# A cross-attention kernel whose first loads are dealt out anew over two DMA queues

## The chip, the core and the metric

One Trainium2 chip, one NeuronCore. The time is device microseconds for one launch of the whole kernel, inputs and output in the chip's memory. All arithmetic is in 32-bit floating point.

## What is computed

Two batches of 2048 tokens with 640 channels attend, with 20 heads of 32 channels, to 154 context rows of 1024 channels. The first 77 rows are text, the last 77 are image prompts with weights of their own; the two softmaxes are separate and their results are added. Then comes the output projection with its bias, and the input is added back.

```
text, ip = ctx[:, :77], ctx[:, 77:]
q    = heads(x @ Wq.T)
k, v = heads(text @ Wk.T), heads(text @ Wv.T)
k_ip, v_ip = heads(ip @ Wk_ip.T), heads(ip @ Wv_ip.T)
out  = softmax(q k.T / sqrt(32)) v  +  softmax(q k_ip.T / sqrt(32)) v_ip
out  = out @ Wo.T + bo + x
```

## The kernel before

Everything lies transposed, channels on the 128 partitions. The 640 channels of a token are five slices of 128 channels (`NC` = 5; "slice k" below), the 1024 context channels eight. Tokens go in blocks of 512 (`TB`); four blocks (`xs[0]` to `xs[3]`) hold the first batch. The 640 query channels are made in five column blocks of Wq (four heads each).

The work on the engines stands in one order, written out by hand as a list of words (`SCHEDULE`, L592): each word emits the instructions of one step, and every engine runs its own in that order. `q.u.h` makes queries of step `u` and block `h` (TensorE, L205, five slices), `cq` scales them (ScalarE, L219), `k` and `v` project keys and values (TensorE, L143, eight slices), `R` makes scores (L241), `K` copies them out, `M`, `S`, `E`, `D`, `I`, `N`, `T` are the steps of the softmax on VectorE, GpSimd and ScalarE, `A` multiplies by the values (L340), and the later words are the output projection. The change does not touch this list. Its first words are `R0.0`, the first scores, and `q.0.1`, which needs x's second block.

Ahead of the list stands a stretch without words, in this order:

- Loads are issued by two engines, SyncE (SP) and ScalarE (ACT); each has a DMA queue of its own. `queues` is the pair `nc.sync, nc.scalar`. `load_x` (L174) takes the next 128-channel slice of x (256 KB); `load_first` (L537) takes one slice of Wq's first column blocks (64 KB a column block); `load_ctx` (L544) takes half of the context (308 KB); `load_w(n)` (L133) takes one block of 512 KB of the key and value weights, in the order Wk, Wk_ip, Wv, Wv_ip for each column block.
- Slice 0 of the first x block comes as two halves of 256 tokens (`SIDES`, L550), 128 KB each.
- TensorE runs five matmuls on zeros (L572). Then it makes the queries of the first block for the first two column blocks together: slice 0 in four matmuls of 256 tokens (L576: column block 0 and 1 on the left half, then on the right half), slices 1 to 4 with 512 tokens (L205). A 32-bit matmul shows as two instructions in the trace.
- ScalarE scales both results. TensorE then projects the first block of Wk, needing both halves of the context, and the first of Wk_ip (`project_kv(0)`, `project_kv(1)`, L143); ScalarE copies each to `kT` (L589), and `R0.0` can begin.

In the kernel before, the halves of x's slice 0 went one to SP and one to ACT, and both column blocks of Wq's slice 0 to ACT, as two transfers of 64 KB, one ahead of and one behind that half of x. Slices 1 and 3 of x went to ACT with Wq's on SP, slices 2 and 4 the other way round. The context went to SP, the first blocks of Wk and Wk_ip to ACT, and x's second block to SP right behind the context.

Of the kernel before, what the change touches and what calls it, by code (L numbers as in the profile page):

```python
# [20 lines left out]
def kernel(  # L21
# [25 lines left out]
    nc = tc.nc  # L47
    P = 128
# [28 lines left out]
    SIDES = slice(0, HT), slice(HT, TB)  # L77
# [12 lines left out]
    xs = [const.tile([P, NC, TB], F32, name=f"x_{n}") for n in range(NHB)]  # L90
# [35 lines left out]
    wlist = [(src, c) for c in range(NC) for src in (WkT, WkipT, WvT, WvipT)]  # L126
    loaded = {}

    def load_w(n, queue=nc.sync):

        src, c = wlist[n]
        w = wslots[n % len(wslots)]
        queue.dma_start(out=w, in_=src[:, ts(c, P)].rearrange("(k p) o -> p k o", p=P))  # L133
        loaded[n] = w

    def keys_in(ps):
# [33 lines left out]
    def load_x(queue=nc.sync):  # L170

        if slices:
            i, k = slices.pop(0)
            queue.dma_start(out=xs[i][:, k], in_=xT[ts(k, P), ts(i, TB)])  # L174
# [358 lines left out]
    queues = nc.sync, nc.scalar  # L533
    slices.pop(0)

    def load_first(queue, k, c, m=3):
        queue.dma_start(  # L537
            out=wq_first[:, k, c:m].rearrange("p c o -> p (c o)"), in_=WqT[ts(k, P), c * P : m * P]
        )

    half = NCC // 2

    def load_ctx(k):
        nc.sync.dma_start(  # L544
            out=wo_ct[:, ds(k * B * LT, half * B * LT)].rearrange("p (k n) -> p k n", k=half),
            in_=ctxT[ds(k * P, half * P), :].rearrange("(k p) n -> p k n", p=P),
        )

    for n, cols in enumerate(SIDES):
        queues[n].dma_start(out=xs[0][:, 0, cols], in_=xT[:P, cols])  # L550
        load_first(nc.scalar, 0, n, n + 1)
    for k in range(1, NC):
        load_x(queues[k % 2])
        load_first(queues[1 - k % 2], k, 0, 2)
    for k in (0, half):
        load_ctx(k)
        load_w(k // half, nc.scalar)
    for _ in range(NC):
        load_x()
    nc.sync.dma_start(out=wq_first[:, :, 2], in_=WqT[:, ts(2, P)].rearrange("(k p) o -> p k o", p=P))  # L560
    for _ in range(NC):
        load_x()
    load_w(2)
    load_w(3)
    for _ in range(NC):
        load_x()
# [236 lines left out]
    for c, stages in enumerate(chains_of):  # L803
        for _, text in stages:
            for _, t in terms(text):
                for h in range(NH):
                    o = int(t[0]), NH * int(t[1]) + h
# [128 lines left out]
```

## Time and profile before

| | |
|---|---|
| median of 3 runs | 501.47 us (501.07 to 502.48) |
| the profiled execution | 502.49 us, of which the span of instructions is 500.7 us |
| TensorE clock granted, mean | 0.997 |
| TensorE matmuls (PE) | 491.0 us busy, 98% of the span |
| VectorE (DVE), GpSimd (POOL), ScalarE (ACT) | 412.7, 370.4, 301.1 us busy |
| DMA | 69.38 MB, mean 139 GB/s; 2.23 MB of it issued by ACT (q10), the rest nearly all by SP (q1) |

Times in the profile are microseconds from the start of the span. PE is TensorE's matmuls, PEld its weight loads, which overlap them. ACTq and SPq are the two engines as issuers of DMAs. `L205` is a line of the kernel. `x24` counts instructions. In brackets stands the idle time ahead of a group and what ended it. In the views of DMA the last number of a row is the time from the issue to the landing. The context lies in the tile `wo_ct` and the first Wq and key weights lie in `aT`, whose room is used otherwise later; the names in the trace are those of the tiles.

### The profile page before, as it was taken

How to read it: one execution, taken by the hardware profiler on the slowest of the kernel's cores; microseconds unless marked ns; L12 is line 12 of the kernel's file. 1: busy time of each engine (PE TensorE's matmuls, PEld its weight loads, DVE VectorE, ACT ScalarE, POOL GpSimd, SP SyncE). 2: the span in 40 equal slices, each digit the busy share in tenths (PEclk: the TensorE clock that was granted, in tenths of full speed). 3: DMA queues.
4: the chain of work that ended last, by engine and by line, in shares of the span. 5: the costliest groups of instructions: out<-in, count | busy, mean ns of one | idle time of the engine just before them, and what ended most of it. 6: DMA issues, size and time to landing. Idle time of an engine off the chain costs nothing.

```text
span 500.7 us, 10393 instructions
## 1 busy us (share of the span) xinstructions
PE 491.0 (98%) x4116; PEld 289.8 (58%) x4116; DVE 412.7 (82%) x418; ACT 301.1 (60%) x929; POOL 370.4 (74%) x158
## 2 busy tenths in 40 slices
PE   7899999999999999999999999999999999999997
PEld 4556648458457557446556654755665586444443
DVE  0039998997999999979979796777899888999886
ACT  1156666987776778768899869586666963100000
POOL 0039998889988989979976697465888999249820
PEclk8999999999999999999999999999999999999999
DMA  8993322341523534497662359444551131511125
GB/s 276 313 283 106 77 61 83 93 112 55 128 64 134 155 119 146 129 329 257 195 200 78 116 133 320 151 126 136 167 173 44 43 108 43 170 42 43 43 84 209
DMA packets 67249, 69.38 MB, mean 139 GB/s; under 512 B 5504, under 2 KB 47232, under 8 KB 67200
## 3 DMA queue, kind: packets, MB, share of 16 engines
q1 hardware_dynamic: 63968, 66.49, 42.4%
q10 hardware_dynamic: 3232, 2.23, 1.5%
q8 instruction: 32, 0.52, 0.4%
q14 instruction: 17, 0.14, 0.1%
HBM read 54.94 MB, written 10.49 MB: 131 GB/s over the span
## 4 chain that ended last, share of the span: by engine, by line
PE 90%; DMA 6%; DVE 2%; issue 0%; ACTq 0%; SPq 0%; ACT 0%; DVEq 0%
PE bank L205 32%; PE bank L887 11%; PE bank L241 10%; PE bank L340 10%; PE bank L498 10%; PE bank L143 8%; PE bank L479 6%; PE bank L508 3%; DMA aT<-in_L_xattn_Wk_ip_dram 3%; DMA acc<-in_x_dram 2%; DMA x<-in_x_dram 1%; DMA aT<-in_L_xattn_Wq_dram 1%; DVE mx L289 1%; DVE mx L292 0%; DVE pb L331 0%
## 5 line engine op out<-in xcount | busy, mean ns | idle before, releaser
L324 POOL TENSOR_TENSOR pb<-pb,rden 128x1848 f32<-128x1848 f32 (+1 forms) x60 | 175.9, 2943 | 25.8 <-DVE rden L319 24.1
L303 POOL TENSOR_TENSOR pb<-pb,mx 128x1848 f32<-128x1848 f32 (+1 forms) x42 | 128.3, 3067 | 63.2 <-PE bank L205 31.5
L205 PE MATMUL bank<-x,wq 128*128 128x512 f32 x280 | 125.8, 598 | 0.1
L289 DVE TENSOR_REDUCE mx<-pb 128x24 f32<-128x1848 f32 (+1 forms) x51 | 93.8, 1849 | 35.7 <-ACT pb L253 35.4
L331 DVE STREAM_TRANSPOSE pb<-pb 128x1920 f32<-128x1920 f32 (+1 forms) x60 | 115.5, 1934 | 6.8 <-POOL pb L324 6.8
L314 DVE TENSOR_REDUCE den<-pb 128x24 f32<-128x1848 f32 (+1 forms) x49 | 91.5, 1873 | 18.5 <-ACT pb L309 15.7
L253 ACT COPY pb<-bank 128x462 f32<-128x462 f32 (+1 forms) x204 | 87.1, 538 | 32.3 <-PE bank L241 31.7
L205 PEld LDWEIGHTS bank<-x,wq 128*128 128x128 f32 x280 | 51.5, 190 | 60.3 <-issue 59.4
L309 ACT ACTIVATE pb<-pb 128x1848 f32<-128x1848 f32 (+1 forms) x42 | 69.4, 1653 | 19.6 <-POOL pb L303 19.5
L277 ACT ACTIVATE pb<-bank,mx 128x77 f32<-128x77 f32 x184 | 53.1, 382 | 11.8 <-DVE mx L292 11.8
L340 PE MATMUL bank<-pb,v 32*32 32x512 f32 x1600 | 55.2, 597 | 0.0
L205 PE MATMUL bank<-x,aT 128*128 128x512 f32 x116 | 53.4, 610 | 0.0
L241 PEld LDWEIGHTS bank<-kT,qT 32*128 32x128 f32 x1024 | 36.5, 184 | 22.6 <-issue 15.5
L277 ACT ACTIVATE pb<-pb,mx 128x77 f32<-128x77 f32 x160 | 47.3, 374 | 0.0
L143 PE MATMUL bank<-wo_ct,aT 128*128 128x154 f32 x320 | 45.7, 297 | 1.2 <-DMA aT<-in_L_xattn_Wk_ip_dram 1.2
L241 PE MATMUL bank<-kT,qT 32*128 32x154 f32 x1024 | 45.8, 307 | 1.0 <-ACT qT L219 0.7
L143 PEld LDWEIGHTS bank<-wo_ct,aT 128*128 128x128 f32 x320 | 42.8, 188 | 4.2 <-issue 2.2
L340 PEld LDWEIGHTS bank<-pb,v 32*32 32x32 f32 x1600 | 30.8, 103 | 21.5 <-issue 9.1
L277 ACT ACTIVATION_READ_ACCUMULATOR pb<-bank,mx 128x1 f32 x144 | 37.0, 260 | 0.0
L205 PEld LDWEIGHTS bank<-x,aT 128*128 128x128 f32 x116 | 22.1, 196 | 24.8 <-issue 22.7
L479 PE MATMUL bank<-aT,wo_ct 128*128 128x512 f32 x80 | 36.4, 595 | 0.0
L219 ACT ACTIVATE qT<-bank 128x512 f32<-128x512 f32 x32 | 19.5, 619 | 27.3 <-PE bank L205 27.3
(83 smaller groups left out, 511.9 us busy)
## 6 DMA issues: line engine op xcount, KB each, us to landing
x<-in_x_dram SPq DMA_DIRECT2D x20, 1280.0 KB, 7.1
out_dram<-acc SPq DMA_DIRECT2D x19, 256.0 KB, 2.7
x<-in_x_dram SPq DMA_DIRECT2D x17, 256.0 KB, 5.9
acc<-in_x_dram SPq DMA_DIRECT2D x16, 256.0 KB, 3.4
out_dram<-x SPq DMA_DIRECT2D x15, 256.0 KB, 2.0
v<-vS SPq DMA_DIRECT2D x160, 20.0 KB, 2.2
aT<-in_L_xattn_Wv_dram SPq DMA_DIRECT2D x5, 512.0 KB, 4.1
aT<-in_L_xattn_Wv_ip_dram SPq DMA_DIRECT2D x5, 512.0 KB, 4.2
```

Source lines behind the costliest of these rows:

```text
L143: nc.tensor.matmul(keys_in(out), loaded[n][:, k, :], cT[:, k, :, t, :], start=(k == 0), stop=(k == NCC - 1))
L205: nc.tensor.matmul(pq, weight_of(q)[:, k, :], xs[place_of(u, h)][:, k, :], start=(k == 0), stop=(k == NC - 1), skip_group_check=loose,)
L241: nc.tensor.matmul(ps[g][:, ts(t, 2 * L)], qTs[(u, h)][g * D : (g + 1) * D, ts(st, P)], kT[g * D : (g + 1) * D, c, b].rearrange("p t l -> ...
L253: nc.scalar.copy(keys_of(u, s)[:, :, g], ps[g][:, : n * 2 * L].rearrange("p (n l) -> p n l", n=n))
L277: nc.scalar.activation(row, row if ps is None else rows_in(ps[g], n)[:, t, x], AF.Exp, bias=maxs[(u, s)][:, *one], accum_out=None if den i ...
L289: nc.vector.tensor_reduce(mx, rows_of(u, s), AX.X, ALU.max, negate=negate)
L303: nc.gpsimd.tensor_tensor(rows_of(u, s), rows_of(u, s), maxs[(u, s)].unsqueeze(3).to_broadcast([P, n, 2, L]), ALU.subtract)
L309: nc.scalar.activation(e, e, AF.Exp)
L314: nc.vector.tensor_reduce(den_of(u, s), rows_of(u, s), AX.X, ALU.add)
L324: nc.gpsimd.tensor_tensor(rows_of(u, s), rows_of(u, s), rdens[(u, s)].unsqueeze(3).to_broadcast([P, n, 2, L]), ALU.mult)
L331: nc.vector.transpose(p, p)
L340: nc.tensor.matmul(pa[r][g * D : (g + 1) * D, :], v4s[q % 2][rows, g, k, :], zones[rows, :, g, k, :], start=(k == 0), stop=(k == NK - 1),)
```

## The change

In the first row, slice 0 of Wq is loaded for both column blocks in one transfer of 128 KB, the first on ACT; the left half of x's slice 0 stays first on SP, the right half is second on ACT. Slices 1 to 4 change sides: x's slices 1 and 3 go to SP and 2 and 4 to ACT, Wq's slices the other way round. Before slice 1 and before slice 3 each queue has the same number of bytes ahead of it: SP has 896 KB in all, ACT 1024 KB, the same totals as before. The first blocks of Wk and Wk_ip go to SP, each behind its half of the context, and so ahead of x's second block. `load_w` loses its argument for the queue. Nothing else changes: what is loaded, where to, and all that the engines compute stay as they were, in the same order.

```diff
-    def load_w(n, queue=nc.sync):
+    def load_w(n):
 
         src, c = wlist[n]
         w = wslots[n % len(wslots)]
-        queue.dma_start(out=w, in_=src[:, ts(c, P)].rearrange("(k p) o -> p k o", p=P))
+        nc.sync.dma_start(out=w, in_=src[:, ts(c, P)].rearrange("(k p) o -> p k o", p=P))
         loaded[n] = w
...
-    for n, cols in enumerate(SIDES):
-        queues[n].dma_start(out=xs[0][:, 0, cols], in_=xT[:P, cols])
-        load_first(nc.scalar, 0, n, n + 1)
+    nc.sync.dma_start(out=xs[0][:, 0, SIDES[0]], in_=xT[:P, SIDES[0]])
+    load_first(nc.scalar, 0, 0, 2)
+    nc.scalar.dma_start(out=xs[0][:, 0, SIDES[1]], in_=xT[:P, SIDES[1]])
     for k in range(1, NC):
-        load_x(queues[k % 2])
-        load_first(queues[1 - k % 2], k, 0, 2)
+        load_x(queues[1 - k % 2])
+        load_first(queues[k % 2], k, 0, 2)
     for k in (0, half):
         load_ctx(k)
-        load_w(k // half, nc.scalar)
+        load_w(k // half)
     for _ in range(NC):
         load_x()
```

The order of issue on each queue, with the size in KB:

| queue | before | after |
|---|---|---|
| SP | x0 left 128, Wq1 128, x2 256, Wq3 128, x4 256, ctx 308, ctx 308, x's second block 5 x 256, ... | x0 left 128, x1 256, Wq2 128, x3 256, Wq4 128, ctx 308, Wk 512, ctx 308, Wk_ip 512, x's second block 5 x 256, ... |
| ACT | Wq0 64, x0 right 128, Wq0 64, x1 256, Wq2 128, x3 256, Wq4 128, Wk 512, Wk_ip 512 | Wq0 128, x0 right 128, Wq1 128, x2 256, Wq3 128, x4 256 |

## The prediction

> **What bounds the kernel now.** I read the cores view first, then the chain of waits, then what TensorE itself waited for, and last the stretch up to 23 us.
>
> ```profile
> core 0: 500.7 us, clock 0.997
> ```
>
> The span is 500.7 us; the profiled execution as a whole took 502.49, so 1.79 us lie around it.
>
> ```profile
> 1.66 4.83 DMA aT<-in_L_xattn_Wq_dram
> ...
> 7.38 12.56 DMA aT<-in_L_xattn_Wk_ip_dram
> ...
> 22.67 1.07 PE bank L241 x24
> 23.73 4.50 PE bank L205 x10
> ...
> 29.98 4.49 PE bank L205 x10
> ...
> 446.63 50.66 PE bank L887 x120
> ```
>
> The chain (start, length, what) runs through two early transfers, a slice of Wq and the first block of Wk_ip. From the first scores, R0.0 at 22.67, it is almost wholly TensorE. What TensorE waited for, longest first (total, times, longest):
>
> ```profile
> PE bank L576 <- DMA aT<-in_L_xattn_Wq_dram: 1.9, 1, 1.9
> PE bank L143 <- DMA aT<-in_L_xattn_Wk_ip_dram: 1.2, 1, 1.2
> ...
> PE bank L498 <- DVE acc L529: 0.7, 1, 0.7
> PE bank L241 <- ACT qT L219: 0.7, 1, 0.7
> ```
>
> So TensorE is the bound, the two transfers are its two longest waits, and both lie ahead of 20 us. A microsecond won before 22.67 should reach the end nearly whole: VectorE, ScalarE and GpSimd take their work from R0.0 and move with it. The timeline of TensorE shows where the early time goes:
>
> ```profile
> 3.54 1.04 PE L576 MATMUL bank<-x,aT 128*128 128x256 f32 x2
> 6.53 1.84 PE L576 MATMUL bank<-x,aT 128*128 128x256 f32 x6 [1.95 <-DMA aT<-in_L_xattn_Wq_dram]
> 8.16 8.49 PE L205 MATMUL bank<-x,aT 128*128 128x512 f32 x16
> 16.49 2.27 PE L143 MATMUL bank<-wo_ct,aT 128*128 128x154 f32 x16
> 19.98 2.37 PE L143 MATMUL bank<-wo_ct,aT 128*128 128x154 f32 x16 [1.22 <-DMA aT<-in_L_xattn_Wk_ip_dram]
> ```
>
> Slice 0 (L576) starts at 3.54 with the first column block of Wq, idles 1.95 us for the second, and goes on at 6.53. Slices 1 to 4 (L205, sixteen passes) take 8.16 to 16.65 without a wait. They are slow for another reason; here are weight loads of two stretches, one per pass, and the windows (last three columns: granted clock, DMA share, GB/s):
>
> ```profile
> 9.01 0.34 PEld L205 LDWEIGHTS bank<-x,aT 128*128 128x128 f32 x1 [0.52 <-issue]
> 9.87 0.34 PEld L205 LDWEIGHTS bank<-x,aT 128*128 128x128 f32 x1 [0.52 <-issue]
> ...
> 12.20 0.19 PEld L205 LDWEIGHTS bank<-x,aT 128*128 128x128 f32 x1 [0.24 <-issue]
> 12.63 0.19 PEld L205 LDWEIGHTS bank<-x,aT 128*128 128x128 f32 x1 [0.24 <-issue]
> ```
>
> ```profile
> 7.00:8.00 1.00, 1.00 (x6) 0.88 (x5) 0.00 (x0) 0.00 (x0) 0.00 (x0) 0.84 1.06 371
> ...
> 11.00:12.00 1.00, 1.00 (x3) 0.44 (x3) 0.00 (x0) 0.00 (x0) 0.00 (x0) 0.95 1.13 310
> ```
>
> A pass takes 0.86 us near 9 and 0.43 near 12: half the clock. A window mean of 0.84 puts the fall to 0.5 at 7.68 (0.32 of the window at half), one of 0.95 puts the return at 11.1. So 3.4 us ran at half clock, a loss of 1.7 us. The fall comes 1.15 us after the idle stretch of 4.58 to 6.53; I take that idle time for its cause.
>
> **The change, part by part.** *The first row.* Every transfer needed for slice 0 to 4 keeps its bytes; they are dealt out again. The queue positions now, from the timeline of the issuing engines and from issue to landing:
>
> ```profile
> 0.73 0.41 ACTq L537 DMA_DIRECT2D aT<-in_L_xattn_Wq_dram  x1
> ...
> 1.18 0.42 SPq L537 DMA_DIRECT2D aT<-in_L_xattn_Wq_dram  x1
> ...
> 1.64 0.43 SPq L174 DMA_DIRECT2D x<-in_x_dram  x1
> ...
> 2.14 0.45 ACTq L174 DMA_DIRECT2D x<-in_x_dram  x1
> ...
> 3.52 0.34 ACTq L537 DMA_DIRECT2D aT<-in_L_xattn_Wq_dram  x1
> ...
> 4.18 0.33 ACTq L174 DMA_DIRECT2D x<-in_x_dram  x1
> ...
> 6.51 0.33 ACTq L537 DMA_DIRECT2D aT<-in_L_xattn_Wq_dram  x1
> ```
>
> ```profile
> aT<-in_L_xattn_Wq_dram ACTq DMA_DIRECT2D x1, 64.0 KB, 2.8
> ...
> aT<-in_L_xattn_Wq_dram SPq DMA_DIRECT2D x1, 128.0 KB, 2.8
> ...
> x<-in_x_dram SPq DMA_DIRECT2D x1, 256.0 KB, 4.7
> ...
> x<-in_x_dram ACTq DMA_DIRECT2D x1, 256.0 KB, 5.3
> ...
> aT<-in_L_xattn_Wq_dram ACTq DMA_DIRECT2D x1, 128.0 KB, 4.8
> ...
> x<-in_x_dram ACTq DMA_DIRECT2D x1, 256.0 KB, 6.4
> ...
> aT<-in_L_xattn_Wq_dram ACTq DMA_DIRECT2D x1, 128.0 KB, 4.7
> ```
>
> The lower fence gives the landings of the upper one, row by row. With the bytes up to and with each transfer: SP had 256 KB in at 3.98 and 512 KB at 6.34; ACT had 64 KB at 3.53, 256 KB at 6.49 (the chain's first row), 512 KB at 7.44, 640 KB at 8.32, 896 KB at 10.58 and all 1024 KB at 11.21. Now both column blocks of Wq's slice 0 are one transfer of 128 KB, first on ACT. From below it lands like the 64 KB in its place (3.53), from above like SP's second transfer of 128 KB (3.98); I take 3.6, nearer the first, since nothing is ahead of it. Its second column block then comes 2.9 us earlier than 6.49, and the 1.95 us of idling go.
>
> Slice 0 is eight passes of 256 columns: 2.1 us, between 1.72 (half of 0.43 each) and 2.45 (six took 1.84). It ends at 5.7. Slice 1 needs 384 KB of each queue. Halfway between the landings above that is 5.16 on SP and 6.97 on ACT; I take 6.1, the middle, so TensorE waits 0.4 us. Slice 2 needs 640 KB of ACT, 8.3 at the latest; TensorE is ready at 6.1 + 1.72 = 7.8 and waits 0.3 (0 to 0.5). Slice 3 needs 768 KB, between 8.32 and 10.58, say 9.45; TensorE is ready at 9.8. Slice 4 needs all 1024 KB, 11.21 at the latest, ready 11.5. With the sixteen passes at full clock, 6.88 us, the queries end at 6.1 + 6.88 + 0.3 = 13.3 (12.6 with no wait at all, 13.9 with every landing at its upper bound), against 16.65. A half-clock stretch would add up to 1.7; I take none, because the waits are now 0.4 and 0.3 us where it was 1.95. ACT's six issues cost ScalarE nothing: it has no work before the queries end. Three issues fewer, and a table load that comes earlier, lie under that same idle time.
>
> *Context, Wk and Wk_ip on SP.* They are now issued by SP, behind its 896 KB, in one row: context, Wk, context, Wk_ip, then x's second block, which ran ahead of Wk_ip on the other queue. Three windows and ACT's line of the first 10 us (packets, MB, share):
>
> ```profile
> 0.00:10.00 10.00, 7.00 (x21) 4.92 (x22) 0.17 (x1) 1.28 (x1) 0.83 (x6) 0.88 0.82 264
> 10.00:20.00 10.00, 8.78 (x32) 4.88 (x30) 0.00 (x0) 1.54 (x4) 0.00 (x0) 0.95 1.11 341
> 20.00:30.00 10.00, 9.00 (x75) 5.70 (x75) 0.00 (x0) 2.09 (x6) 0.00 (x0) 1.00 0.96 301
> ```
>
> ```profile
> q10 hardware_dynamic: 1130, 1.10, 32.0%
> ```
>
> An issue waits until the transfer eight places ahead in the order of all issues has landed: ACT's at 3.52 for the 64 KB that landed at 3.53, that at 6.51 for the block that landed at 6.49. By this count Wk's issue now waits for slice 1 of Wq (about 6.1) and Wk_ip's for slice 2 of x (8.3), while SP's queue still has its own slices to move; so its queue doesn't run dry.
>
> 2.64 MB are in by 10 us. Up to both halves of context and Wk it is 3048 KB, 3.12 MB; up to Wk_ip 3.65 MB; up to x's second block 4.96 MB. From 10 us on they move at 341 GB/s (both queues) or 301 (SP alone in the last window). A landing comes after the bytes: ACT had moved 1.10 MB by 10.0 and its 1024 KB (1.05 MB) landed at 11.21, so I add 1.5 us, an estimate from this one pair, 1.2 at least. Context and Wk land at 12.9 to 13.1, just before the queries end at 13.3; Wk_ip at 14.5 to 14.9. Wk's projection, 2.27 us, ends at 15.6, so Wk_ip is there and the wait of 1.22 us goes. From the start of Wk_ip's projection to R0.0 it is 22.67 - 19.98 = 2.69 us, unchanged. R0.0 starts at 13.3 + 2.27 + 2.69 = 18.3 instead of 22.67: 4.4 us earlier. The second block of x (4.96 MB) lands at 18.3 to 19.2; its first use was 1.06 us after R0.0, now 19.4, and its last slice is used 3.6 us later still. It is next in line to be late and has little to spare.
>
> *What follows on SP.* Its issues for x's third block, Wq's third column block, Wv and so on come in the same order. SP waited for Wk_ip before it could issue some of them; that wait falls earlier too. The third block (with Wq's columns 6.60 MB) is in at 24.7 even at 301 GB/s, and needed at 29.98 - 4.4 = 25.6.
>
> The sum: 1.95 + 1.7 + 1.22 = 4.9 removed, less 0.4 and 0.3 of new waits, gives 4.2; by the end times it is 4.4. I take 4.3, with 3.8 and 4.8 as ends: 502.49 - 4.3 = 498.2, between 497.7 and 498.7. The three runs took 502.48, 501.47 and 501.07, so the profiled execution is 1.02 us above the median. I read that as the half-clock stretch falling more or less on the path from run to run, and do not subtract it again; if it has another cause, the result is 1 us lower.
>
> **The rivals.** *Half a clock all the same.* The fall at 7.68 may come from something other than the idle stretch, or the new waits (up to 6.97 - 5.7 = 1.3 us at slice 1) may suffice for it. For it: the wait that I blame was itself only 1.95 us. Against it: TensorE would be idle 0.7 us in all. Then 1.7 us come back: 499.9 (499.4 to 500.4). The Trainium skill ("TensorE: Matmul & The Clock Gate", the table in "Why this matters for your kernels") warns only of idle gaps above about 3 us between bursts; by that rule the gap here was harmless and this rival would hold. The trace speaks against the figure, since the clock fell after a gap of 1.95 us.
>
> *The first slices come no earlier.* If 128 KB at once land as late as the second column block did, the start is paced as before and only Wk_ip's 1.22 us and a part of the first wait are won: about 501. Against it stand the 128 KB on SP that landed 2.8 us after issue.
>
> *SP alone is too slow, and x's second block is late (slower).* The place is the first use of that block, 1.06 us after R0.0. Of 4.96 MB, 2.32 are left at 10 us. The last slice is used now at 23.73 + 3.6 = 27.3; less 1.5 for landing, SP would have to need 15.8 us for them, 147 GB/s, before anything is lost against today. At 120 GB/s it would land at 30.8, and the time would be 506.0. Against it: 301 GB/s with SP alone. The Trainium skill ("DMA: Bandwidth & Descriptors", "Rules for kernel authors") holds that spreading over issuing engines brings no bandwidth, which also speaks against this rival; 301 against 341 here says a little is lost.
>
> **How the numbers follow.** About 0.3%, 1.5 us, is what a measurement of this kernel can tell from no change, so faster means below 499.97. Forecast 0.60; still better (below 497.7) 0.04; half clock 0.24, two thirds of it below 499.97 because the median may lie 1 us lower; no earlier slices 0.07; slower 0.05. Faster: 0.60 + 0.04 + 0.16 = 0.80; same: 0.08 + 0.07 = 0.15; slower 0.05. The range takes the forecast, 1 us below it for the median, and the half-clock rival: 496.8 to 500.4.
>
> **What would show it.** In the changed kernel TensorE's wait on L576 for Wq should be gone and that on L143 for Wk_ip too; L205's sixteen passes should stand 0.43 apart from the first; R0.0 should start near 18.3; the windows up to 12 us should hold a clock near 1. I am wrong if passes 0.86 apart remain (first rival), if slice 0 still starts its second half after 5 us (second), or if TensorE waits for x within L205 after 18 us (third). If R0.0 comes 4 us earlier and the end does not, a later stage had its own bound.

## The result, and the profile after

The median fell from 501.47 us to 498.26 us (497.75 to 499.36): a ratio of 0.9938, 95% interval 0.9921 to 0.9956. The forecast was 498.2 in 496.8 to 500.4. The sum behind it held less well than its total: the start won 1.1 us less than forecast, and about as much of the profiled time that the forecast started from (1.2 us) belonged to no edit.

The cores view, and what TensorE waited for in the changed kernel (the longest that are left, apart from the start):

```profile
core 0: 496.3 us, clock 1.000
```

```profile
PE bank L205 <- DMA aT<-in_L_xattn_Wq_dram: 0.7, 1, 0.7
PE bank L241 <- ACT qT L219: 0.7, 1, 0.7
PE bank L143 <- DMA aT<-in_L_xattn_Wk_ip_dram: 0.4, 1, 0.4
```

The waits of 1.9 us for Wq and 1.2 us for Wk_ip became 0.7 and 0.4. The two late waits on L498 for VectorE are not there either; that is taken up below. The timeline of TensorE and two weight loads:

```profile
3.53 2.93 PE L576 MATMUL bank<-x,aT 128*128 128x256 f32 x8
7.18 7.10 PE L205 MATMUL bank<-x,aT 128*128 128x512 f32 x16 [0.72 <-DMA aT<-in_L_xattn_Wq_dram]
14.12 2.27 PE L143 MATMUL bank<-wo_ct,aT 128*128 128x154 f32 x16
16.75 2.37 PE L143 MATMUL bank<-wo_ct,aT 128*128 128x154 f32 x16 [0.36 <-DMA aT<-in_L_xattn_Wk_ip_dram]
19.44 1.07 PE L241 MATMUL bank<-kT,qT 32*128 32x154 f32 x24 [0.31 <-ACT kT L589]
```

```profile
8.97 0.19 PEld L205 LDWEIGHTS bank<-x,aT 128*128 128x128 f32 x1 [0.24 <-issue]
9.40 0.19 PEld L205 LDWEIGHTS bank<-x,aT 128*128 128x128 f32 x1 [0.24 <-issue]
```

Slice 0 runs in one piece; the sixteen passes of slices 1 to 4 take 7.10 us instead of 8.49, 0.43 apart. R0.0 starts at 19.44 instead of 22.67: 0.98 us from the earlier start of slice 1, 1.39 from the faster passes, 0.86 from the shorter wait for Wk_ip, 3.23 in all. The chain shows what sets this stretch now:

```profile
2.14 6.20 DMA x<-in_x_dram
...
8.35 8.36 DMA aT<-in_L_xattn_Wk_ip_dram
```

It goes from x's slice 2, for whose landing the issue of Wk_ip waits, to the landing of Wk_ip at 16.71. TensorE's work does not appear in it before 16.75.

### The profile page after: what moved, and what is told of

Its sections match the earlier page's. It is cut to its first block, busy times and chain, and to the rows that moved or that the text cites. A ratio compares the mean times of both kernels' runs of the same rounds, so it can differ in the third digit from the quotient of the medians.

```text
span 496.3 us, 10391 instructions
## 1 busy us (share of the span) xinstructions
PE 489.6 (99%) x4116; PEld 289.1 (58%) x4116; DVE 412.9 (83%) x418; ACT 300.9 (61%) x929; POOL 370.4 (75%) x158
## 3 DMA queue, kind: packets, MB, share of 16 engines
q10 hardware_dynamic: 1008, 1.18, 0.7%
## 4 chain that ended last, share of the span: by engine, by line
PE 96%; DMA 3%; ACT 0%; ACTq 0%; DVE 0%; issue 0%; DVEq 0%
PE bank L205 34%; PE bank L887 11%; PE bank L340 11%; PE bank L241 11%; PE bank L498 10%; PE bank L143 9%; PE bank L479 7%; PE bank L508 3%; DMA aT<-in_L_xattn_Wk_ip_dram 2%; DMA x<-in_x_dram 1%; ACTq L537 0%; ACT qT L219 0%; ACT pb L253 0%; ACTq L551 0%; DVE acc L830 0%
## 5 line engine op out<-in xcount | busy, mean ns | idle before, releaser
L205 PE MATMUL bank<-x,aT 128*128 128x512 f32 x116 | 52.0, 597 | 0.7 <-DMA aT<-in_L_xattn_Wq_dram 0.7
L340 PEld LDWEIGHTS bank<-pb,v 32*32 32x32 f32 x1600 | 30.5, 103 | 21.8 <-issue 9.2
L205 PEld LDWEIGHTS bank<-x,aT 128*128 128x128 f32 x116 | 21.3, 189 | 24.9 <-issue 24.5
```

The source lines that it names most:

```text
L205: nc.tensor.matmul(pq, weight_of(q)[:, k, :], xs[place_of(u, h)][:, k, :], start=(k == 0), stop=(k == NC - 1), skip_group_check=loose,)
L340: nc.tensor.matmul(pa[r][g * D : (g + 1) * D, :], v4s[q % 2][rows, g, k, :], zones[rows, :, g, k, :], start=(k == 0), stop=(k == NK - 1),)
```

## The experiments

All ratios are to the kernel before, run on the same chip in turn. The place to read in each profile is the start of R0.0.

**The kernel before, again.** No edit.

> The kernel before, profiled a second time, against itself. Between the first profiles the span fell by 4.4 us, the start of R0.0 only by 3.2 (22.67 to 19.44); the other 1.2 us lie where TensorE waited for VectorE (0.7 and 0.3 us on L498). Theory: those late waits come and go from execution to execution and are no part of the change; then this profile has a span between 499.3 and 500.7 and may lack them, with R0.0 again at 22.5 to 22.8. Rival: they belong to the order of the work in the kernel before; then they stand again, 0.6 us or more together, and the change removed them by its earlier start. Both expect the half-clock stretch of 3.4 us again if the idle stretch ahead of 6.5 us causes it.

Measured: 501.57 us against 501.59, ratio 0.9996 (0.9984 to 1.0009). The second profile, cores and TensorE's timeline, and one window of a microsecond (the third number from the end is the granted clock):

```profile
core 0: 499.9 us, clock 0.999
```

```profile
7.16 2.93 PE L576 MATMUL bank<-x,aT 128*128 128x256 f32 x6 [2.57 <-DMA aT<-in_L_xattn_Wq_dram]
9.88 7.31 PE L205 MATMUL bank<-x,aT 128*128 128x512 f32 x16
...
23.06 1.07 PE L241 MATMUL bank<-kT,qT 32*128 32x154 f32 x24 [0.31 <-ACT kT L589]
```

```profile
8.00:9.00 1.00, 1.00 (x3) 0.76 (x3) 0.00 (x0) 0.38 (x1) 0.00 (x0) 1.00 1.06 393
```

R0.0 starts at 23.06, later than in the first profile (and than the 22.5 to 22.8 expected), and the span is shorter; the waits on L498 are absent. So they come and go, as the theory had it. The other part of its expectation held in another form: after an idle stretch of 2.57 us the rest of slice 0 ran at half clock (six passes of 256 columns in 2.93 us, 1.84 in the first profile), and the slow passes ended a little after 10 us. The granted clock stands at 1.00 in that window all the same: the clock changes kept with this trace begin with the rise to full clock at 10.4 us, and the column reads 1.00 ahead of the first of them. In this stretch the lengths of the passes tell the clock, not that column.

**Only the first row.** `load_w(k // half, nc.scalar)` put back; the rest as changed.

> Only the first row is dealt out anew; Wk and Wk_ip stay on the issue of ScalarE. Theory (the start of R0.0 sets the end, and it waits for the later of the queries and Wk_ip): the queries end near 14.3 us as in the changed kernel, but Wk_ip lands at 19 to 20 as before, so TensorE waits 2.5 to 3.5 us there and R0.0 starts at 22 to 22.7: the time falls by 0 to 0.7 us. Rival (the parts add up): the new row alone is worth 0.98 + 1.39 = 2.4 us, time 499.1.

Measured: 502.75 us, ratio 1.0024 (1.0010 to 1.0038). Slower, which neither expected. In TensorE's timeline:

```profile
7.26 7.11 PE L205 MATMUL bank<-x,aT 128*128 128x512 f32 x16 [0.51 <-DMA aT<-in_L_xattn_Wq_dram]
17.63 4.45 PE L143 MATMUL bank<-wo_ct,aT 128*128 128x154 f32 x32 [3.26 <-DMA aT<-in_L_xattn_Wk_dram]
```

The queries end near 14.3 us as in the changed kernel, but now Wk itself lands at 17.5 (15.3 in the first profile of before). SP had x's second block issued from 7.33 us, a microsecond earlier than before, and it shares the DMA engines with Wk on the other queue, which would explain the delay; no run takes it apart. The parts do not add up: the first row alone gains nothing. This profile is of its fastest run (501.10). Its twelve runs lie in three groups by mean granted clock: 501.1 to 501.4 us at 1.000, 502.6 to 502.8 at 0.996 to 0.997, and 503.4 to 504.3 at 0.992 to 0.993. A mean of 0.993 over 502 us is a loss of up to 3.5 us, so the slower runs are those in which the clock was down for longer; where in the span it was down, and whether the wait of 3.26 us brings it about, is not shown.

**Only the weights on SP.** In the kernel before:

```diff
-        load_w(k // half, nc.scalar)
+        load_w(k // half)
```

> Only Wk and Wk_ip go to SP ahead of x's second block; the first row stays as before. Theory: the queries end at 16.65 as before, Wk_ip is there by 17 to 18.9, so its wait of 1.22 us is gone and R0.0 starts at 21.3 to 21.8: the time falls by 0.9 to 1.3 us, to 500.2 to 500.6. The half-clock stretch stays. Rival (the parts add up): this part is worth 0.86 us, time 500.6; the two theories part on the first row alone.

Measured: 500.17 us, ratio 0.9979 (0.9963 to 0.9994): a fall of 1.4 us. The runs lie between 498.15 and 502.39. The profile is of one of the longer ones (501.57). TensorE waits there for neither Wk nor Wk_ip, but R0.0 starts at 22.94, not at the 21.3 to 21.8 expected:

```profile
7.18 2.93 PE L576 MATMUL bank<-x,aT 128*128 128x256 f32 x6 [2.62 <-DMA aT<-in_L_xattn_Wq_dram]
9.90 8.50 PE L205 MATMUL bank<-x,aT 128*128 128x512 f32 x16
18.25 4.38 PE L143 MATMUL bank<-wo_ct,aT 128*128 128x154 f32 x32
22.94 1.07 PE L241 MATMUL bank<-kT,qT 32*128 32x154 f32 x24 [0.31 <-ACT kT L589]
```

Behind an idle stretch of 2.62 us the rest of slice 0 and three to four passes of slice 1 ran at half clock. That this is what spreads the other runs is not shown.

**The same, with the idle stretch filled.**

```diff
                 pq[:, cols], wq_first[:, 0, c], xs[0][:, 0, cols], start=(n == 0), stop=False, skip_group_check=True
             )
+            if n == c == 0:
+                for _ in range(6):
+                    nc.tensor.matmul(banks[0][:, :P], warm, warm, start=True, stop=True)
```

> The same with six more matmuls on zeros between the first and the second matmul of slice 0, so that TensorE is busy while it waits for the second column block. No load is moved. Theory (the idle 1.95 us cause the half clock): the clock stays at 1.0, the sixteen passes of slices 1 to 4 take about 7.0 us instead of 8.5, the queries end near 15.2 and R0.0 starts near 20.2: 1.2 to 1.5 us less than with the weights on SP alone, 498.9 to 499.3. Rival (a half-clock stretch comes anyway near 8 us): passes of 0.86 us remain, and the time is that of the kernel without the extra matmuls, or up to 0.3 us more.

Measured: 498.82 us, ratio 0.9944 (0.9929 to 0.9959), runs within 498.16 to 499.56.

```profile
4.39 1.75 PE L581 MATMUL bank<-pb 128*128 128x128 f32 x12
6.60 1.56 PE L576 MATMUL bank<-x,aT 128*128 128x256 f32 x6 [0.46 <-DMA aT<-in_L_xattn_Wq_dram]
8.00 7.03 PE L205 MATMUL bank<-x,aT 128*128 128x512 f32 x16
...
19.56 1.07 PE L241 MATMUL bank<-kT,qT 32*128 32x154 f32 x24 [0.31 <-ACT kT L592]
```

No load was moved. R0.0 starts 3.4 us earlier than in the profile without the filling: 0.6 us because the second column block happened to come earlier (6.60 against 7.18), and 2.8 because the passes behind it ran at full clock (1.56 and 7.03 us, against 2.93 and 8.50). In the medians it is 1.35 us, and the two intervals do not overlap. The fastest runs of both kernels are alike (498.16 and 498.15), so the idle stretch does not cost this in every execution. But it is the idle stretch, and not something that comes anyway, that keeps the clock at half.

**The changed kernel with slice 0 of Wq split again.**

```diff
-    load_first(nc.scalar, 0, 0, 2)
+    load_first(nc.scalar, 0, 0, 1)
     nc.scalar.dma_start(out=xs[0][:, 0, SIDES[1]], in_=xT[:P, SIDES[1]])
+    load_first(nc.scalar, 0, 1, 2)
```

> The changed kernel with slice 0 of Wq in two transfers of 64 KB again, the second behind the right half of x on ScalarE's queue; all else as changed. Theory (the one transfer of 128 KB removes the idle stretch, and the idle stretch keeps the clock at half): the second column block lands at 5.5 to 6.5 us, TensorE idles 1 to 2 us within slice 0, passes of 0.86 us return in slices 1 to 4, and R0.0 starts 1 to 3 us later than 19.44: 499.3 to 501.3. Rival (the order of the queues for slices 1 to 4 does it): slice 1 still starts near 7.2 us, no pass takes 0.86, and the time is that of the changed kernel, 498.3 within 0.3.

Measured: 499.48 us, ratio 0.9953 (0.9935 to 0.9970). The idle stretch is back at half its size, and slow passes with it:

```profile
5.61 2.92 PE L577 MATMUL bank<-x,aT 128*128 128x256 f32 x6 [0.97 <-DMA aT<-in_L_xattn_Wq_dram]
8.32 7.77 PE L205 MATMUL bank<-x,aT 128*128 128x512 f32 x16
...
20.62 1.07 PE L241 MATMUL bank<-kT,qT 32*128 32x154 f32 x24 [0.31 <-ACT kT L590]
```

R0.0 is 1.2 us later than in the changed kernel. The times agree with that; their interval overlaps that of the changed kernel.

**The changed kernel with its waits filled.** Three such matmuls behind each half of slice 0.

> The changed kernel with three matmuls on zeros behind the left half of slice 0 and three behind the right half, where TensorE waits for the right half of x and for slice 1 of Wq. Theory (what spread is left in the changed kernel, 497.75 to 499.36, is the clock coming up sooner or later): the runs lie closer together, within 1.0 us, and the median falls by 0 to 0.6 us, to 497.7 to 498.3; the wait for Wk_ip, 0.4 us, takes up the rest. Rival (the spread has its place elsewhere, as in the landing of Wk_ip): median and spread stay as they are, or the median rises by the 0.3 us by which the extra matmuls may overrun the waits.

Measured: 499.29 us, ratio 0.9956 (0.9941 to 0.9972), runs from 498.50 to 501.10. The theory fails: the spread did not shrink. The median did not fall either; by the ratios it is 0.9 us above that of the changed kernel, with intervals that overlap.

```profile
3.62 2.08 PE L576 MATMUL bank<-x,aT 128*128 128x256 f32 x4
5.49 1.40 PE L580 MATMUL bank<-pb 128*128 128x128 f32 x6
6.72 1.03 PE L576 MATMUL bank<-x,aT 128*128 128x256 f32 x4
7.59 0.83 PE L580 MATMUL bank<-pb 128*128 128x128 f32 x6
```

The first half of slice 0 took 2.08 us at half clock; the right half of x had landed at 4.99 by then, so that the filling, from 5.49, had nothing to bridge and delayed the second half to 6.72 (5.25 in the changed kernel). The matmuls on zeros helped only where nothing useful could run.

**A candidate with the same number of rows ahead.** In the changed kernel, x's slice 0 whole on SP, Wq's slice 0 on ACT, then x and Wq in turn:

```diff
-    nc.sync.dma_start(out=xs[0][:, 0, SIDES[0]], in_=xT[:P, SIDES[0]])
+    nc.sync.dma_start(out=xs[0][:, 0], in_=xT[:P, :TB])
     load_first(nc.scalar, 0, 0, 2)
-    nc.scalar.dma_start(out=xs[0][:, 0, SIDES[1]], in_=xT[:P, SIDES[1]])
     for k in range(1, NC):
-        load_x(queues[1 - k % 2])
-        load_first(queues[k % 2], k, 0, 2)
+        load_x(queues[k % 2])
+        load_first(queues[1 - k % 2], k, 0, 2)
```

> A candidate: slice 0 of x whole, as one transfer of 256 KB on SP beside Wq's slice 0 on ScalarE's queue, then slices 1 to 4 with x and Wq in turn, x's slice 1 on ScalarE's queue. Each queue then has the same number of rows (128 a transfer) ahead of every slice, not the same bytes. Theory (the two queues are served row by row: in the changed kernel SP had 256 rows and 384 KB in at 4.98, ScalarE's queue 384 rows and 384 KB only at 7.05): both parts of slice 1 land by 6.2, TensorE starts slice 0 at 3.8 to 4.5, waits less than 0.4 us for slice 1, and the queries end at 13.0 to 13.8 instead of 14.28. Wk_ip's landing then binds, so the time falls by 0 to 0.5 us, to 497.8 to 498.3. Rival (served by bytes): slice 1 lands at 7.0 as before, TensorE has idled longer ahead of slice 0, and the time is 0.3 to 1.5 us more.

Measured: 499.81 us, ratio 0.9964 (0.9950 to 0.9977). In the changed kernel slice 1's parts, issued at 1.18 and 1.65, landed after (first row x on SP, second Wq on ACT):

```profile
x<-in_x_dram SPq DMA_DIRECT2D x1, 256.0 KB, 3.8
...
aT<-in_L_xattn_Wq_dram ACTq DMA_DIRECT2D x1, 128.0 KB, 5.4
```

that is at 4.98 and 7.05, with 384 KB on each queue. In the candidate both were issued at 1.18:

```profile
x<-in_x_dram ACTq DMA_DIRECT2D x1, 256.0 KB, 4.5
...
aT<-in_L_xattn_Wq_dram SPq DMA_DIRECT2D x1, 128.0 KB, 4.3
```

They landed together, at 5.7 and 5.5, again with 384 KB on each queue but also 256 rows on each. So the queues are served by rows (packets) rather than by bytes. The windows of the changed kernel say the same. From 3.5 to 3.9 us (packets, MB, share; q1 is SP's queue, q10 ACT's):

```profile
q1 hardware_dynamic: 45, 0.09, 68.0%
q10 hardware_dynamic: 41, 0.04, 29.5%
```

The packets are nearly equal, the bytes are not. The Trainium skill ("DMA: Bandwidth & Descriptors", "Queues, rings and completion order") has each DMA engine take turns between queues packet by packet; the trace agrees. The candidate is slower for another reason: Wq's slice 0 landed at 4.85, and TensorE idled 1.35 us before it and ran slice 0 at half clock.

**Wk_ip back on ACT.** In the changed kernel, `load_w(k // half, queues[k // half])`.

> The changed kernel with Wk_ip alone back on the issue of ScalarE, behind its 1024 KB; context and Wk stay on SP. Theory (what lands first is a matter of what is queued ahead, row by row: Wk_ip has 1024 rows of 512 bytes on a queue of its own against context, Wk, and x's second block on the other): Wk_ip lands by 15 to 17 and Wk, which now shares the engines with it, 1 to 2 us later than its 13.2; R0.0 starts within 0.5 us of 19.44, the time 498.0 to 498.8. Rival (a block on ScalarE's queue is starved by SP, as in the kernel with only the first row changed, where Wk landed at 17.5): Wk_ip lands at 18 or later, and the time rises by 1.3 us or more, to 499.6 and above.

Measured: 499.53 us, ratio 0.9954 (0.9937 to 0.9971). Wk_ip landed at 15.6 and TensorE waited for neither block. But in its profile Wq's slice 0 landed at 4.16 instead of 3.5, slice 0 ran at half clock, and R0.0 started at 20.37. The theory on the landings holds (Wk at 14.27, 1.1 us later); the time lies between the theory's and the rival's, and what of it is due to the edit is left open. Its profile has the two waits on L498 again, 0.7 and 0.2 us.

**The changed kernel again, and two more candidates.** The first has both halves of x's slice 0 on SP (384 rows there up to and with slice 1's part, 256 on ACT), the second has Wk_ip on ACT as well.

```diff
     nc.sync.dma_start(out=xs[0][:, 0, SIDES[0]], in_=xT[:P, SIDES[0]])
     load_first(nc.scalar, 0, 0, 2)
-    nc.scalar.dma_start(out=xs[0][:, 0, SIDES[1]], in_=xT[:P, SIDES[1]])
+    nc.sync.dma_start(out=xs[0][:, 0, SIDES[1]], in_=xT[:P, SIDES[1]])
     for k in range(1, NC):
-        load_x(queues[1 - k % 2])
-        load_first(queues[k % 2], k, 0, 2)
+        load_x(queues[k % 2])
+        load_first(queues[1 - k % 2], k, 0, 2)
```

> The changed kernel once more, beside the two candidates on one chip. Theory (TensorE starts at half clock, and the clock comes up at a moment that differs from execution to execution): slices 0 and 1 show passes at half clock for a longer or shorter time than in its first profile, R0.0 starts between 19.0 and 21, and the end is R0.0 plus 476.8 to 478.1. Rival (the start is fixed by the landings): R0.0 again within 0.2 us of 19.44. Time 497.9 to 498.8 in both.

> A candidate: both halves of x's slice 0 on SP, Wq's slice 0 alone ahead on ScalarE's queue, x's slice 1 behind it; slices in turn from there; weights on SP as in the changed kernel. Ahead of slice 1 SP has 384 rows and ScalarE's queue 256 (in the changed kernel 256 and 384). Theory (served row by row): the right half of x lands near 4.0 instead of 5.2, slice 1 by 6.2 instead of 7.05, so slice 0 begins at 3.5 and nothing waits up to the projections; 0.4 to 0.9 us less than the changed kernel, 497.4 to 497.9, as far as the landing of Wk_ip (16.7) lets it. Rival (what is won in the queries is lost waiting for Wk_ip): within 0.3 us of the changed kernel.

> The same with Wk_ip issued by ScalarE behind its slices, where it landed at 15.6 instead of 16.7 when tried alone. Theory: no wait for Wk_ip, and the gain of the new row comes through: 0.6 to 1.2 us less than the changed kernel, 497.1 to 497.7. Rival (Wk and Wk_ip share the engines, and the context and Wk now land after the queries end): a wait for Wk of 0.3 us or more takes its place, and the time is that of the changed kernel or above.

Measured: 498.22, 498.38 and 498.54 us; ratios 0.9924 (0.9906 to 0.9943), 0.9926 (0.9908 to 0.9944) and 0.9931 (0.9915 to 0.9948). No candidate beats the change. The changed kernel's second profile:

```profile
3.76 3.51 PE L576 MATMUL bank<-x,aT 128*128 128x256 f32 x8 [0.21 <-DMA aT<-in_L_xattn_Wq_dram]
...
18.95 1.07 PE L241 MATMUL bank<-kT,qT 32*128 32x154 f32 x24 [0.31 <-ACT kT L589]
```

Slice 0 took 3.51 us instead of 2.93, at half clock up to its last pass, and R0.0 started earlier all the same, because the landings were kinder (Wq's slice 1 at 6.17 instead of 7.05, Wk_ip at 16.2 instead of 16.7). R0.0 is in neither expected place: 0.05 us below the theory's range, and 0.5 from the first profile, so the start is not fixed. The first candidate's timeline:

```profile
6.19 7.03 PE L205 MATMUL bank<-x,aT 128*128 128x512 f32 x16
...
14.80 1.32 PE L143 MATMUL bank<-wo_ct,aT 128*128 128x154 f32 x8 [0.37 <-DMA wo_ct<-in_ctx_dram]
16.59 2.37 PE L143 MATMUL bank<-wo_ct,aT 128*128 128x154 f32 x16 [0.47 <-DMA aT<-in_L_xattn_Wk_ip_dram]
19.27 1.07 PE L241 MATMUL bank<-kT,qT 32*128 32x154 f32 x24 [0.31 <-ACT kT L589]
```

Slice 1 begins a microsecond earlier and without a wait, as the rows had it, and the microsecond is handed back waiting for the second half of the context and for Wk_ip. With Wk_ip on ACT the wait moves to Wk (1.51 us). In both candidates it is the landings of the context and the key weights that set R0.0. In both, SP has the 384 rows, and now SP's part of slice 1 is the late one: it landed at 5.5 and 6.2, ACT's at 4.9 in both. So the late part goes with the rows and not with ACT as issuer. Each of these transfers has 128 rows, so that rows and the number of transfers were not told apart by the landings; the packets of the window above speak for the rows.

**x's second block held back.** One line ahead of its loads in the changed kernel:

```diff
+    nc.gpsimd.tensor_copy(xs[1][:, :, 0:1], wslots[1][:, :NC, 0:1])
     for _ in range(NC):
         load_x()
```

> The changed kernel with x's second block held back: its loads wait for a small copy on GpSimd, which is idle then, and the copy waits for Wk_ip to land. By 13 us 3.72 MB have moved in the changed kernel, all that is needed up to Wk_ip (3.65 MB); it landed only at 16.71, when 4.98 MB had moved. Theory (the transfers behind it on the queue run ahead on some of the DMA engines while others are still at Wk_ip): with nothing behind it, Wk_ip lands at 14.5 to 15.3, the wait of 0.4 us for it is gone, R0.0 starts near 19.0, and x's second block lands at 19 to 20.5, so that TensorE waits 0 to 1 us for it after R0.0; the time is within 0.7 us of the changed kernel. Rival (the 512-byte rows of Wk_ip are slow by themselves): it lands at 16.2 or later, and as x's second block then lands at 21 or later, TensorE waits 1 to 3 us for it: 499.2 to 501.2.

Measured: 498.69 us, ratio 0.9935 (0.9915 to 0.9955). With nothing behind it Wk_ip landed at 16.57. With the block behind it, it landed at 16.71 and 16.2 in the two profiles of the changed kernel. The theory, 14.5 to 15.3, fails. What had moved by 16 us, with nothing issued beyond Wk_ip:

```profile
DMA packets 4715, 4.28 MB, mean 267 GB/s; under 512 B 238, under 2 KB 4203, under 8 KB 4715
```

4.28 MB, not the 3.65 of my count. The row of the context in the trace reads 616.0 KB for each of its two transfers; I had taken it for both. **Half of the context is 616 KB, not 308**, in the prediction and in the table of the change as well. The rival's landing held; its cause (slow short rows) was not needed, and was not excluded. Its price was less, and the time lies below its range: x's second block made the queries after R0.0 take 5.31 us instead of 4.56.

## Why the prediction was right or wrong

| step | forecast | measured |
|---|---|---|
| slice 0 starts | 3.6 | 3.53 |
| slice 0 takes | 2.1 | 2.93 |
| slice 1 starts | 6.1 | 7.18 |
| queries end | 13.3 | 14.28 |
| Wk_ip lands, wait for it | 14.5 to 14.9, none | 16.71, 0.36 |
| R0.0 starts | 18.3 | 19.44 |
| won by then | 4.4 (4.3 taken) | 3.23 |
| profiled execution | 498.2 | 498.10 |

*Right, as to mechanism.* The 1.95 us of idling within slice 0 went with the one transfer of 128 KB, which landed 2.8 us after issue as its nearest row had it; the half clock in slices 1 to 4 went with the idling (shown by the filling, and agreeing with it by the splitting); Wk_ip no longer follows x's second block. TensorE did not wait for that block, so the slower rival did not come.

*Mis-sized: slice 1.* I put its landing halfway between the two queues' landings (6.1) and took the other end, 6.97, for a bound. It was 7.05: with the same bytes ahead, but 384 rows against 256, ACT's part is the late one.

*Mis-sized: the bytes up to Wk_ip.* 616 KB were missing from the count. With them, 4.28 MB less the 2.64 of the first 10 us at 341 to 301 GB/s, plus the same 1.5 us, give 16.3 to 16.9; measured 16.71. This is why the changed kernel stands against the DMA now, and why neither candidate could use an earlier end of the queries.

*Wrong, and by luck it covered the first two.* The profiled execution of before was 1.02 us above the median. I read that as the half clock falling more or less on the path. It was the end of the kernel: span less start of R0.0, from the cores view and the timeline of each profile:

| kernel | span | R0.0 | difference |
|---|---|---|---|
| before, first profile | 500.7 | 22.67 | 478.0 |
| before, second profile | 499.9 | 23.06 | 476.8 |
| only the first row | 499.3 | 22.39 | 476.9 |
| only the weights on SP | 499.8 | 22.94 | 476.9 |
| idle stretch filled | 496.3 | 19.56 | 476.7 |
| Wk_ip back on ACT | 498.4 | 20.37 | 478.0 |
| changed, two profiles | 496.3, 495.8 | 19.44, 18.95 | 476.9, 476.9 |

From R0.0 on the kernel takes 476.7 to 476.9 us, or 478.0 in the two profiles that have the waits on L498 (0.7 and 0.2 to 0.3 us). So whatever moves R0.0 moves the end by as much, as forecast, and the first profile of before carried 1.2 us that belong to no edit. The profiles that are not in the table give 476.8 to 476.9, but for x's second block held back: 477.6, with its 0.75 us of longer queries behind R0.0. Against its own time the fall was 4.4 us; between the medians it is 3.2, as much as R0.0 won from first profile to first profile. That the two agree to the tenth is chance, for R0.0 differs by 0.4 to 0.5 us between two profiles of one kernel. The prediction had said that with another cause than the half clock the result would be 1 us lower. There was another cause, and the result was not lower, because the start won a microsecond less. That 498.26 lies so near 498.2 is luck. What makes the waits on L498 come and go was not tried.

*The first rival* (half clock all the same) falls as to its cause, but the clock does not rise at a fixed time, and the prediction left out that it is at half from the start. Slice 0 of the changed kernel ran partly or almost wholly at half clock (2.93 and 3.51 us, forecast 2.1); in the first profile the later landing of slice 1 hid it. The clock changes kept with the traces, which agree with the lengths of the passes, sort the profiles by the idle time that TensorE had before its clock was up. In eight it idled at most 0.21 us at a time on the first loads, and full clock came at 4.9 to 7.3 us. In five it idled 0.65 to 2.62 us, and full clock came at 9.8 to 12.9. In the first profile of before the clock was up at 4.3, and behind the 1.95 us of idling it was at half again from 7.7 to 11.1. In these last six profiles some passes of slices 1 to 4 were slow; where the gap was filled none was.

The Trainium skill ("TensorE: Matmul & The Clock Gate", the table in "Why this matters for your kernels") warns of idle gaps above about 3 us as a cause of a falling clock. The first profile of before had the fall after 1.95 us, and the profile with only the first row had none after 3.26 us, so that the length of a gap alone does not decide here. In the other five of the six the clock had not risen yet when the gap came.

## What to carry to other kernels

Look for the instruction from which the rest of the kernel takes a constant time, and read every edit of the start by when that instruction begins; a second profile of the unchanged kernel shows how constant it is. Count the bytes of a transfer from its own row, and the rows as well as the bytes that lie ahead of it on its queue. Two edits at the start can be worth less than nothing and something apart, and more than their sum together, since the later of two arrivals decides.

## What was not expected of the hardware

TensorE's first ten passes (128 columns, on zeros) took 2.50 us in every profile and stood 0.21 us apart; behind them, in the kernel with the filling, the same passes stood 0.11 apart once the clock was up. So it started at half clock each time, and stayed there for different times: up to 5.4 us in one profile of the changed kernel and 6.9 in the other, up to 4.3 and 10.4 in the two of the kernel before, and up to 12.9 with only the weights on SP. The column of the granted clock read 1.00 in those stretches; of the profiles quoted here it showed a fall in the first 20 us only in the first of before.

Two queues with equal bytes, but 256 rows on one and 384 on the other, delivered their parts of one slice 2.1 us apart in the first profile of the changed kernel (1.3 in the second), and 0.3 apart once their rows were equal.
